# A sort and its roots one step earlier, a batch of keys behind a sum, and a different last pair, in a graph-attention kernel

## The chip, the core and the metric

The kernel runs on one core of a Trainium2 chip. The metric is the device time of one launch in microseconds (us). One execution of the program was taken by the hardware profiler; all durations of single instructions come from it.

The engines are called as the profile calls them: PE is TensorE's matmul pipeline and PEld its weight loads, DVE is VectorE, ACT is ScalarE, POOL is GpSimd, and SP is SyncE, which here only issues DMAs. A name such as L985 is line 985 of the kernel before.

## What is computed

The layer takes 2708 rows `x` of 1024 numbers and a 0/1 adjacency matrix `adj` of 2708 x 2708, in which about four entries of a row are one.

```python
h = maximum(layernorm(x), 0)
q = h @ Wq.T + bq ;  k = h @ Wk.T + bk ;  v = h @ Wv.T + bv
z = (q @ k.T) / sqrt(1024) * adj
z = where(z == 0, -10000, z)
out = x + relu(softmax(z, axis=1) @ v)
```

Since a row has few neighbours, the kernel computes no dense scores. It finds the indices of the ones in each row of `adj`, gathers the neighbours' rows of `h`, scores them one by one, and forms the weighted sum `u` of the gathered rows. The two weight matrices of the scores are combined once, M = Wq^T Wk (scaled), so that a query row is h M and its score with a neighbour is a dot product with that neighbour's h; the values' product is taken last, on the sum u.

## The kernel before, in words

**Tiles.** The rows form 22 tiles of 128 (`NT` = 22); the last, tile 21, has 20 rows and is called the rest tile. `EARLY` = 11 divides them: tiles 0 to 10 are the first part, 11 to 21 the second. Within each part the rows are sorted by their number of neighbours, so that a tile of the sorted order needs as many gathers as its longest row. A "row tile" below is a tile in sorted order; the table `ptab` holds, for each sorted row, its neighbours' indices and its own number in `x`.

**Matmul units.** After the combination of the weights (to about 105 us), TensorE works through 20 units, each for two tiles: units 0 to 9 form queries, of tiles (0,1), (2,3), (4,5), (6,7), (8,9), and then (11,12) to (19,20); tile 10's query stands alone after unit 4. Units 10 to 19 form output rows from u, in the order (8,7), (6,5), (4,3), (2,0), (1,9), (15,14), (13,12), (16,17), (20,10), (18,19); tile 11's output stands alone at the end (`alone`). A unit (`multiply`, L940) multiplies the two tiles' 256 rows by a 1024 x 1024 matrix as seven products of half-size blocks instead of eight (a Strassen form, which costs block sums ahead and behind). Its operands are transposes of the rows (TensorE, L355), copies of these (ACT, L645: a11, a12, a22) and block sums (DVE L649, or POOL where that is named: s1 to s4). Its results are c11, c22, c12 and c21, taken from PSUM: for queries by L982 (ACT), L985 and L988 (DVE sums) and L993 (ACT); for outputs by L1010 to L1026, where ACT applies the relu. Copies of partial products that later products are added to are L917, L920 and the like on ACT. The first two products of unit n+1 are issued inside unit n (`opened`), ahead of its last.

**Hooks.** Between the products of unit n the code calls `after(0)` to `after(6)`. There the next unit's rows, transposes and block sums are issued, and there the preparation of later tiles is woven in: the dictionary `steps_at` (L696) lists, by (unit, hook), short steps that `follow` (L270) carries out:

- s: statistics of tiles (DVE, L212); r: the root, eight small GpSimd instructions that form scale and bias from them (L232 to L239); a: the normalisation with relu, applied in place (ACT, L248)
- h: the rows' store to HBM (`h_dram`, GpSimd's queue, L255) and their addition to a running sum (GpSimd, L257); k: the store with the addition left for later; +: that addition
- p: "size", a pass of ACT over a tile's adjacency rows that counts its ones (L320); it also makes the next load into that buffer possible, as there are three
- f: the index search in a tile's adjacency (DVE, four instructions of L330); i, j: search, and the keys of a batch of four tiles (`listed`, L332 on; DVE L342 and those after it); e: size, search and keys; here an f for the batch's last tile is not given its keys
- c: counts of neighbours in the first part, up to a table of hot bits by degree (DVE, L595 to L603); o: the sort of the first part, two matmuls against constant matrices, a scan and some sums on DVE (L606 to L622), which gives each row its place
- w: one indirect DMA for each of tiles 0 to 10 puts the rows' table entries into their places in HBM (GpSimd, L564), and the table is read back (L576)

The second part's counts and sort stand in unit 3's hooks 2 and 3 (L1126 to L1130), without letters; `entered` then puts its eleven entries, reads the table back and gathers tiles 11 and 12 of h (L541), the rows for unit 5's queries. The second sort's result is also needed for the attention stream.

**Attention.** A generator (`attention`, L850) yields after each small piece, and `advance` pulls pieces in proportion to the matmuls issued. For each row tile it asks for the neighbours' rows (`ask`, `fill`: gathers of GpSimd, L541, into a set of buffers), fetches the query rows (L543), scores (DVE L785), forms weights, and sums (DVE L838). If `near(t)` holds, because the tile's output unit is at most two units away, u stays on chip (`held`); otherwise it is stored to `u_dram` (L847) and read again by `load_rows` (L1070).

**Outputs.** `add_x` adds the rows of x to a finished output tile with an indirect DMA of GpSimd (L1003), and `scatter` writes them to their rows of the output (L739). The rest tile has been sorted behind tile 20, and its output is one row repeated (tile 20's last), which goes through a row of HBM (`tail_dram`, L1021) to `tail` (L1041): load, add x, scatter. For tile 11 (L1226 on) x is gathered ahead into y, DVE adds the relu of its product to y, and two half-row scatters write it (L1219).

**Order of instructions.** ACT and DVE issue in program order until unit 5, from there DVE alone; GpSimd does so until step w, where `pooled.close()` ends it. The other engines, and these outside those stretches, are ordered by a scheduler that goes by dependencies and priorities; `tc.issue_after(x)` holds what stands under it behind instruction x. So where a step's instructions land is read from each engine's order of instructions, not from the source alone. SP and POOL each issue DMAs from their own queue, in their own order.

The lines of the steps, where unit 1 is tiles (2,3) and its successor, unit 2, is tiles (4,5):

```python
(1, 4): "r8 e15",
(1, 6): "f16", (2, 1): "f17 c", (2, 2): "p16 a8", (2, 3): "h8 f18 p17",
(2, 4): "o s10 p18", (2, 5): "f19 r10 w", (2, 6): "f20 f21 a10 k10 p19",
...
def near(t):
    return any(t in unit[1:] for unit in units[:now[0] + 3] if unit[0] == "o")
```

Of the kernel before, what the change touches and what calls it, by code (L numbers as in the profile page):

```python
# [15 lines left out]
ALU = mybir.AluOpType  # L16
AX = mybir.AxisListType

P = 128
# [4 lines left out]
SLOTS = 16  # L24
# [33 lines left out]
def tile_preln_masked_attention(  # L58
# [157 lines left out]
    def moments(t):  # L216
# [4 lines left out]
        nc.scalar.activation(junk, xs[i], AF.Copy, scale=-1.0 / (ROOT * D), accum_out=mv[:, i, 0:1])  # L221
        nc.scalar.activation(junk, xs[i], AF.Square, scale=1.0 / ROOT, bias=mv[:, i, 0:1], accum_out=mv[:, i, 1:2])

    def root(first):

        group, xs, mv = normed.pop(first)
        G = len(group)
        r = stat.tile([P, 5, 4], FT, tag="r", name="r")
        mean, var = mv[:, :G, 0], mv[:, :G, 1]
        down = float(ROOT) if first < LIGHT else -1.0  # L230
        eng = nc.gpsimd
        eng.tensor_scalar(r[:, 0, :G], var, EPS, None, op0=ALU.add)  # L232
        eng.tensor_tensor(r[:, 1, :G], r[:, 0, :G], minus[:, :G], op=ALU.pow)
        eng.tensor_tensor(r[:, 2, :G], r[:, 0, :G], r[:, 1, :G], op=ALU.mult)
        eng.tensor_tensor(r[:, 2, :G], r[:, 2, :G], r[:, 1, :G], op=ALU.mult)
        eng.tensor_scalar(r[:, 2, :G], r[:, 2, :G], -0.5, 1.5, op0=ALU.mult, op1=ALU.add)
        eng.tensor_tensor(r[:, 3, :G], r[:, 2, :G], r[:, 1, :G], op=ALU.mult)
        eng.tensor_scalar(r[:, 2, :G], mean, down, None, op0=ALU.mult)
        eng.tensor_tensor(r[:, 4, :G], r[:, 2, :G], r[:, 3, :G], op=ALU.mult)  # L239
        normed[first] = group, xs, r  # L240

    def apply(first, only=range(4)):
# [27 lines left out]
    def follow(steps):  # L270

        for step in steps.split():
            first, *only = step[1:].split(".")
            first, *last = first.split("-")
            first = int(first or 0)
            if step[0] == "s":
                stats(range(first, int(last[0] if last else first) + 1))
            elif step[0] == "m":
                moments(first)
            elif step[0] == "r":  # L280
                root(first)
            elif step[0] == "a":
                apply(first, *[range(int(o[0]), int(o[-1]) + 1) for o in only])
            elif step[0] in "hk":
                keep(first, step[0] == "h")
            elif step[0] == "+":
                owe(first)
            elif step[0] == "p":
                counted(first)
            elif step == "c":  # L290
                counts(0, EARLY)
            elif step == "o":
                sort(0, EARLY)
            elif step == "w":
                pooled.close()
                with tc.issue_after(put(0, EARLY).ins):
                    back.append(reload(0, EARLY))
            else:
                if step[0] == "e":
                    counted(first)  # L300
                if step[0] != "j":
                    found(first)
                if step[0] != "i":
                    listed(first)
# [372 lines left out]
    def natural_rows(n):  # L677
# [16 lines left out]
    nc.vector.tensor_scalar(large[:, 1:2], large[:, 1:2], 250000.0 / D, None, op0=ALU.is_gt)  # L694

    steps_at = {(0, 0): "s4-5 e9", (0, 1): "r4 +0 +1 +2 f10", (0, 3): "p10 i11", (0, 4): "j11 a4 p11", (0, 5): "h4 +3 s6-7 e12",  # L696
                (0, 6): "r6 f13", (1, 1): "f14", (1, 2): "p13 a6", (1, 3): "h6 s8-9 p14", (1, 4): "r8 e15",
                (1, 6): "f16", (2, 1): "f17 c", (2, 2): "p16 a8", (2, 3): "h8 f18 p17",
                (2, 4): "o s10 p18", (2, 5): "f19 r10 w", (2, 6): "f20 f21 a10 k10 p19", (3, 2): "p20", (3, 3): "p21"}

    slots, free = [], []

# [145 lines left out]
        done.add(t)  # L848

    def attention(order):  # L850
        for t in order[:3]:
            ask(t)

        fill()
# [33 lines left out]

    def near(t):

        return any(t in unit[1:] for unit in units[:now[0] + 3] if unit[0] == "o")

    def advance(us):

# [110 lines left out]
    def o_results(ta, tb):  # L1005
        ya = work.tile([P, D], FT, tag="q", name=f"y_{ta}", bufs=4)
        yb = work.tile([P, D], FT, tag="q", name=f"y_{tb}", bufs=4)

        def c11(X):
            nc.scalar.activation(ya[:, lo], X, AF.Relu)  # L1010
# [14 lines left out]
        def c21(Y):  # L1025
            nc.scalar.activation(yb[:, lo], Y, AF.Relu)  # L1026
            send(add_x(yb, tb))
            sent.append((yb, tb))

        return c11, c22, c12, c21  # L1030

# [9 lines left out]
    def tail(t):  # L1041
        n = tiles[t][1]
        y = work.tile([P, D], FT, tag="q", name=f"y_{t}", bufs=4)
        nc.sync.dma_start(y[:n], tail_dram.to_broadcast([n, D]))
        add_x(y, t, n)
        scatter(y, t, n)
# [67 lines left out]
    for n, unit in enumerate(units):  # L1114
# [8 lines left out]
        results = (q_results if kind == "q" else o_results)(ta, tb)  # L1123

        def after(i):
            if (n, i) == (3, 2):  # L1126
                counts(EARLY, NT)
            if (n, i) == (3, 3):
# [38 lines left out]
                follow(steps_at[n, i])  # L1167
            if (n, i) == (3, 4):
                searched()
            if nxt is None and i == 1:  # L1170
                while alone not in done:
                    advance(1.0)
                r, = load_rows(("o", alone))
                single["turned"] = turned(r, "alone")
# [50 lines left out]

    y = work.tile([P, D], FT, tag="q", name="y_alone", bufs=4)  # L1226
    send(gather(y, x, alone, SLOTS, P))
    tail(NT - 1)
    uT, (X, Z), p1 = single["turned"], single["banks"], single["first"]
    add_block(Z, uT[:, 0:4, :], T[:, 0])  # L1230
    add_block(Z, uT[:, 4:8, :], M[:, 1, 1])
# [188 lines left out]
```

## Time and profile before

| what | value |
|---|---|
| time, median of 3 runs (lowest to highest) | 678.27 us (677.11 to 678.88) |
| the profiled execution: time, span in the profile | 678.58 us, 676.8 us |
| mean granted clock of TensorE over the span | 0.991 |
| instructions | 6390 |
| TensorE's products (L904), the two largest groups | 320 matmuls each, 145.3 us and 144.1 us |
| gathers of neighbours' h (POOL L541) | 104, 124.6 us |
| scores (DVE L785), sums (DVE L838) | 112.6 us, 98.7 us |
| index search (DVE L330) | 88 instructions, 74.4 us |
| HBM | 161.38 MB read, 45.46 MB written, 306 GB/s over the span |

How to read it. The page's first part gives, for each engine, how long it was busy and the share of the span. A list of waits has lines of the form "waiting instruction <- what ended its wait: us, number of waits, longest"; the left side is the engine, its operand and its line, the right side the releaser. A table of stretches has a row for each window "from:to" in us from the span's start: its length, then each engine's busy time with the number of instructions, then TensorE's granted clock (1.00 is full speed), the share of the DMA engines in use, and GB/s. A listing in order of time has the start, the duration, the engine, the line, the operation, its output and inputs with their shapes, and in brackets the idle time of that engine before it with its releaser. "Issue" as a releaser means that nothing the profile shows was waited for.

The slices of the page, 40 of 16.9 us each, give the course of the whole:

```profile
PE   7999999998998999999999999999999999999894
POOL 2559990756475764576656265775684776862123
PEclk9999999999999999999999999999999999999898
```

Each digit is a busy share in tenths, and 9 is 90% or more. TensorE's dips after the first slice lie in slices 10, 13, 38 and in the last.

### The profile page before, as it was taken

The numbers are of one execution on the slowest core, as the hardware profiler recorded it, in microseconds if no ns is written. First come the engines' busy times: TensorE is split into PE (matmuls) and PEld (weight loads), VectorE is DVE, ScalarE is ACT, GpSimd is POOL, SyncE is SP. The second block draws the span as 40 slices with busy tenths as digits, with TensorE's granted clock in tenths as the row PEclk, the third lists the DMA queues.
The fourth block names the chain that finished last, engine by engine and source line by source line (L and its number), as shares of the span: only waits on it lengthen the run. The fifth ranks groups of instructions, "written<-read, shape, count | busy, mean of one in ns | idle before, by whom it ended". The sixth has DMA issues, their size and how long they took to land.

```text
span 676.8 us, 6390 instructions
## 1 busy us (share of the span) xinstructions
PE 655.5 (97%) x1768; PEld 334.8 (49%) x1768; DVE 525.7 (78%) x1010; ACT 266.3 (39%) x399; POOL 402.1 (59%) x397
## 2 busy tenths in 40 slices
PE   7999999998998999999999999999999999999894
PEld 4777765443544444444444444444444444444441
DVE  5999879989798402999878999788799989989001
ACT  3467985673727212243241232342322343332210
POOL 2559990756475764576656265775684776862123
PEclk9999999999999999999999999999999999999898
DMA  8997989698464997699899999998997899883534
GB/s 343 407 367 258 369 308 373 220 403 292 161 243 152 380 329 294 201 367 313 302 335 357 374 414 382 300 311 254 312 294 199 241 316 309 250 277 81 162 99 137
DMA packets 62452, 194.29 MB, mean 287 GB/s; under 512 B 9721, under 2 KB 10073, under 8 KB 61514
## 3 DMA queue, kind: packets, MB, share of 16 engines
q0 software_dynamic: 34608, 109.77, 49.9%
q1 hardware_dynamic: 26794, 80.89, 32.2%
q10 hardware_dynamic: 1008, 3.15, 1.2%
q8 instruction: 16, 0.26, 0.1%
q14 instruction: 26, 0.21, 0.1%
HBM read 161.38 MB, written 45.46 MB: 306 GB/s over the span
## 4 chain that ended last, share of the span: by engine, by line
PE 74%; DVE 10%; DMA 7%; issue 4%; ACT 3%; POOL 1%; POOLq 0%; ACTq 0%; SPq 0%; DVEq 0%
PE ps L904 32%; PE psy L904 23%; PE ps_y L414 6%; PE ps_x L414 4%; PE ps_z L414 4%; PE pt L355 4%; DMA adj<-in_adj_dram 3%; DVE u L838 2%; DVE at L330 2%; DVE junk L785 1%; DVE s L649 1%; DMA y<-in_x_dram,tab 1%; ACT sized L320 1%; DMA u_dram<-u 1%; DMA out_dram<-y,tab 1%
## 5 line engine op out<-in xcount | busy, mean ns | idle before, releaser
L541 POOL DMA_INDIRECT g<-h_dram,tab x104 | 124.6, 1198 | 51.3 <-issue 22.8
L904 PE MATMUL psy<-wlow,s 128*128 128x512 f32 x320 | 145.3, 596 | 0.0
L904 PE MATMUL ps<-M,a 128*128 128x512 f32 x320 | 144.1, 593 | 0.1
L785 DVE SCALAR_TENSOR_TENSOR junk<-g,pq 128x1024 uint8<-128x1024 f32 x92 | 112.6, 1223 | 2.0
L838 DVE SCALAR_TENSOR_TENSOR u<-g,coef,u 128x1024 f32<-128x1024 f32 x77 | 98.7, 1282 | 8.9 <-ACT u L830 7.3
L904 PEld LDWEIGHTS psy<-wlow,s 128*128 128x128 f32 x320 | 59.8, 192 | 67.4 <-issue 67.4
L904 PEld LDWEIGHTS ps<-M,a 128*128 128x128 f32 x320 | 59.3, 190 | 68.0 <-issue 67.7
L904 PE MATMUL psy<-wlow,a 128*128 128x512 f32 x160 | 73.9, 606 | 3.1 <-DVE q L985 2.7
L330 DVE FIND_INDEX8 at<-ones,adj 128x8 uint32<-128x685 f32 (+1 forms) x88 | 74.4, 864 | 0.0
L904 PE MATMUL ps<-M,s 128*128 128x512 f32 x160 | 71.9, 592 | 0.0
L904 PE MATMUL ps<-wlow,s 128*128 128x512 f32 x160 | 71.9, 592 | 0.0
L1003 POOL DMA_INDIRECT y<-in_x_dram,tab x21 | 37.2, 1769 | 57.9 <-ACT y L1018 28.4
L320 ACT ACTIVATE sized<-adj 128x2708 uint8<-128x2708 f32 (+1 forms) x22 | 54.2, 2464 | 7.2 <-DMA adj<-in_adj_dram 7.1
L904 PEld LDWEIGHTS psy<-wlow,a 128*128 128x128 f32 x160 | 30.7, 194 | 43.5 <-issue 35.9
L904 PEld LDWEIGHTS ps<-wlow,s 128*128 128x128 f32 x160 | 30.4, 190 | 38.3 <-issue 38.0
L904 PEld LDWEIGHTS ps<-M,s 128*128 128x128 f32 x160 | 30.3, 190 | 37.3 <-issue 37.3
L257 POOL TENSOR_TENSOR hsum<-hsum,x 128x1024 f32<-128x1024 f32 (+1 forms) x17 | 40.3, 2370 | 0.4
L649 DVE TENSOR_TENSOR s<-a,pt 128x512 f32<-128x512 f32 x40 | 25.6, 680 | 17.2 <-ACT a L645 9.7
L543 POOL DMA_INDIRECT pq<-q_dram,tab x11 | 15.5, 1411 | 33.2 <-DVE junk L785 21.2
L645 ACT COPY a<-pt 128x512 f32<-128x512 f32 x60 | 33.2, 593 | 4.2 <-PE pt L355 4.2
L541 POOL DMA_INDIRECT M<-h_dram,tab x20 | 25.9, 1293 | 11.1 <-issue 4.9
L739 POOL DMA_INDIRECT out_dram<-y,tab x21 | 24.5, 1164 | 9.8 <-issue 5.8
(229 smaller groups left out, 888.6 us busy)
## 6 DMA issues: line engine op xcount, KB each, us to landing
adj<-in_adj_dram SPq DMA_DIRECT2D x21, 1354.0 KB
x<-in_x_dram SPq DMA_DIRECT2D x21, 512.0 KB
h_dram<-x POOLq DMA_DIRECT2D x21, 512.0 KB
u_dram<-u POOLq DMA_DIRECT2D x15, 512.0 KB
or<-u_dram SPq DMA_DIRECT2D x15, 512.0 KB
q_late<-q SPq DMA_DIRECT2D x10, 512.0 KB
pq<-q_late POOLq DMA_DIRECT2D x10, 512.0 KB
g<-in_wv_dram SPq DMA_DIRECT2D x16, 256.0 KB
```

Source lines behind the costliest of these rows:

```text
L257: nc.gpsimd.tensor_add(hsum[:n], hsum[:n], xt[:n])
L320: nc.scalar.activation(sized[:n], a[:n, :, :PW], AF.Abs, accum_out=total[:n, t:t + 1])
L330: nc.vector.max_index(at[:n, t - first_t, g, :], ones[:n, 0:8], a[:n, g, :])
L355: nc.tensor.transpose(pt[:, c, :], xt[:, k * P:(k + 1) * P], ident)
L414: mm = nc.tensor.matmul(bank, a_tile(o + H * a[0], a[1], i), b(o), start=first and o == 0, stop=(o == H - 1), skip_group_check=True)
L541: return nc.gpsimd.indirect_dma_start(out=dst, out_offset=None, in_=src, in_offset=off, bounds_check=N - 1, oob_is_err=False)
L645: nc.scalar.copy(ops[name], bank)
L649: step = (eng or nc.vector).tensor_tensor(ops[name], a, b, op=op)
L785: chained(lambda: nc.vector.scalar_tensor_tensor(junk, g_of[t][s], 1.0, tq[t], op0=ALU.mult, op1=ALU.mult, accum_out=zall[:, t, s:s + 1]))
L838: chained(lambda: nc.vector.scalar_tensor_tensor(u, g_of[t][s], coef[:, at[t][s]:at[t][s] + 1], u, op0=ALU.mult, op1=ALU.add))
L904: mm = nc.tensor.matmul(bank, a[:, c, :], b[:, c, :], start=False, stop=(c == 3), skip_group_check=True)
L1003: return nc.gpsimd.indirect_dma_start(out=y[:n], out_offset=None, in_=x, in_offset=off, compute_op=ALU.add)
```

## The change

The change has five parts.

1. **The sort of the first part stands earlier, and the roots ahead of the entries.** The counts (c) move from hook (2,1) to (1,6), and the sort with tile 10's statistics (o s10) from (2,4) to the beginning of hook (2,2), through a new dictionary `steps_ahead`, so that they stand ahead of what else that hook issues. Tile 10's root (r10) moves from (2,5) to (2,3), and step w from (2,5) to (2,3), behind the index search of tile 18 and the size of tile 17. `h8` moves behind w in the same hook. Tile 10's apply (a10) moves from (2,6) to (2,4), ahead of the size of tile 18, and its store (k10) to (2,5). `root` notes its last instruction in `rooted`, and w issues the eleven entries behind the last root noted, and the reload behind the last entry.
2. **The keys of a batch stand behind a sum.** Step e15 (size, search and keys) becomes p15 and i15 in hook (1,4), and the keys (j15) come a hook later, in (1,5). Between the two stands the sum L985 of that unit.
3. **The attention stream asks for the gathers of its first two tiles at once, not of three.** The third is asked for when the stream comes to it.
4. **Tile 11's u stays on chip.** `near` is true for `alone`, so that neither the store to `u_dram` nor the load takes place.
5. **The last pair and the rest tile.** For the last output pair, tiles 18 and 19, x is gathered into ya and yb ahead of the products, one DVE instruction for each quarter of the result takes the relu of it and adds x, and the scatters follow directly; ACT's relus and the adding DMAs go. `tail`, for the rest tile, is called in hook 3 of the unit behind the one that holds tile 20, which is unit 19, and not after unit 19's end.

The arithmetic of every tile is the same otherwise.

```diff
@@ -221,6 +221,8 @@
         nc.scalar.activation(junk, xs[i], AF.Copy, scale=-1.0 / (ROOT * D), accum_out=mv[:, i, 0:1])
         nc.scalar.activation(junk, xs[i], AF.Square, scale=1.0 / ROOT, bias=mv[:, i, 0:1], accum_out=mv[:, i, 1:2])
 
+    rooted = []
+
     def root(first):
 
         group, xs, mv = normed.pop(first)
@@ -236,7 +238,7 @@
         eng.tensor_scalar(r[:, 2, :G], r[:, 2, :G], -0.5, 1.5, op0=ALU.mult, op1=ALU.add)
         eng.tensor_tensor(r[:, 3, :G], r[:, 2, :G], r[:, 1, :G], op=ALU.mult)
         eng.tensor_scalar(r[:, 2, :G], mean, down, None, op0=ALU.mult)
-        eng.tensor_tensor(r[:, 4, :G], r[:, 2, :G], r[:, 3, :G], op=ALU.mult)
+        rooted.append(eng.tensor_tensor(r[:, 4, :G], r[:, 2, :G], r[:, 3, :G], op=ALU.mult))
         normed[first] = group, xs, r
 
     def apply(first, only=range(4)):
@@ -293,7 +295,9 @@
                 sort(0, EARLY)
             elif step == "w":
                 pooled.close()
-                with tc.issue_after(put(0, EARLY).ins):
+                with tc.issue_after(rooted[-1].ins):
+                    entry = put(0, EARLY)
+                with tc.issue_after(entry.ins):
                     back.append(reload(0, EARLY))
             else:
                 if step[0] == "e":
@@ -694,9 +698,10 @@
     nc.vector.tensor_scalar(large[:, 1:2], large[:, 1:2], 250000.0 / D, None, op0=ALU.is_gt)
 
     steps_at = {(0, 0): "s4-5 e9", (0, 1): "r4 +0 +1 +2 f10", (0, 3): "p10 i11", (0, 4): "j11 a4 p11", (0, 5): "h4 +3 s6-7 e12",
-                (0, 6): "r6 f13", (1, 1): "f14", (1, 2): "p13 a6", (1, 3): "h6 s8-9 p14", (1, 4): "r8 e15",
-                (1, 6): "f16", (2, 1): "f17 c", (2, 2): "p16 a8", (2, 3): "h8 f18 p17",
-                (2, 4): "o s10 p18", (2, 5): "f19 r10 w", (2, 6): "f20 f21 a10 k10 p19", (3, 2): "p20", (3, 3): "p21"}
+                (0, 6): "r6 f13", (1, 1): "f14", (1, 2): "p13 a6", (1, 3): "h6 s8-9 p14", (1, 4): "r8 p15 i15", (1, 5): "j15",
+                (1, 6): "f16 c", (2, 1): "f17", (2, 2): "p16 a8", (2, 3): "r10 f18 p17 w h8",
+                (2, 4): "a10 p18", (2, 5): "f19 k10", (2, 6): "f20 f21 p19", (3, 2): "p20", (3, 3): "p21"}
+    steps_ahead = {(2, 2): "o s10"}
 
     slots, free = [], []
 
@@ -848,7 +853,7 @@
         done.add(t)
 
     def attention(order):
-        for t in order[:3]:
+        for t in order[:2]:
             ask(t)
 
         fill()
@@ -888,7 +893,7 @@
 
     def near(t):
 
-        return any(t in unit[1:] for unit in units[:now[0] + 3] if unit[0] == "o")
+        return t == alone or any(t in unit[1:] for unit in units[:now[0] + 3] if unit[0] == "o")
 
     def advance(us):
 
@@ -1005,6 +1010,8 @@
     def o_results(ta, tb):
         ya = work.tile([P, D], FT, tag="q", name=f"y_{ta}", bufs=4)
         yb = work.tile([P, D], FT, tag="q", name=f"y_{tb}", bufs=4)
+        if (ta, tb) == o_pairs[-1]:
+            return ends(ya, ta, yb, tb)
 
         def c11(X):
             nc.scalar.activation(ya[:, lo], X, AF.Relu)
@@ -1026,6 +1033,32 @@
             nc.scalar.activation(yb[:, lo], Y, AF.Relu)
             send(add_x(yb, tb))
             sent.append((yb, tb))
+
+        return c11, c22, c12, c21
+
+    def ends(ya, ta, yb, tb):
+
+        send(gather(ya, x, ta, SLOTS, P))
+        gather(yb, x, tb, SLOTS, P)
+
+        def joined_x(y, cols, a):
+            nc.vector.scalar_tensor_tensor(y[:, cols], a, 0.0, y[:, cols], op0=ALU.max, op1=ALU.add)
+
+        def c11(X):
+            joined_x(ya, lo, X)
+
+        def c22(Y, p5):
+            nc.vector.tensor_add(p5, Y, p5)
+            joined_x(yb, hi, p5)
+
+        def c12(Z, u2):
+            nc.vector.tensor_add(u2, Z, u2)
+            joined_x(ya, hi, u2)
+            scatter(ya, ta, P)
+
+        def c21(Y):
+            joined_x(yb, lo, Y)
+            scatter(yb, tb, P)
 
         return c11, c22, c12, c21
 
@@ -1123,6 +1156,8 @@
         results = (q_results if kind == "q" else o_results)(ta, tb)
 
         def after(i):
+            if (n, i) in steps_ahead:
+                follow(steps_ahead[n, i])
             if (n, i) == (3, 2):
                 counts(EARLY, NT)
             if (n, i) == (3, 3):
@@ -1167,6 +1202,8 @@
                 follow(steps_at[n, i])
             if (n, i) == (3, 4):
                 searched()
+            if i == 3 and units[n - 1][0] == "o" and NT - 2 in units[n - 1][1:]:
+                tail(NT - 1)
             if nxt is None and i == 1:
                 while alone not in done:
                     advance(1.0)
@@ -1225,7 +1262,6 @@
 
     y = work.tile([P, D], FT, tag="q", name="y_alone", bufs=4)
     send(gather(y, x, alone, SLOTS, P))
-    tail(NT - 1)
     uT, (X, Z), p1 = single["turned"], single["banks"], single["first"]
     add_block(Z, uT[:, 0:4, :], T[:, 0])
     add_block(Z, uT[:, 4:8, :], M[:, 1, 1])
```

## The prediction

> **What bounds the kernel.** I read the busy shares first, then TensorE's own waits, then the clock in short stretches around each wait, then each engine's order of time there.
>
> ```profile
> PE 655.5 (97%) x1768; PEld 334.8 (49%) x1768; DVE 525.7 (78%) x1010; ACT 266.3 (39%) x399; POOL 402.1 (59%) x397
> ```
>
> TensorE is busy 97% of the span, and the chain that ended last is TensorE for most of it. The change takes no matmul away, so it can win only TensorE's idle time, clock lost behind that idle time, and what follows the last matmul. TensorE's list of waits has three of over 1 us that the change can reach:
>
> ```profile
> PE psy L904 <- DVE q L985: 2.7, 1, 2.7
> PE pt L355 <- DMA or<-u_dram: 2.6, 1, 2.6
> PE ps_in L611 <- ACT a L645: 2.0, 1, 2.0
> ```
>
> The stretches around them (us; then busy time of PE, PEld, DVE, ACT, POOL; granted clock; DMA share; GB/s):
>
> ```profile
> 163.00:166.00 3.00, 0.31 (x2) 0.14 (x2) 2.76 (x17) 0.58 (x1) 1.48 (x7) 1.00 1.00 354
> 166.00:170.00 4.00, 4.00 (x6) 1.70 (x7) 4.00 (x11) 0.00 (x0) 0.00 (x0) 0.57 0.42 163
> 206.00:209.00 3.00, 0.97 (x5) 0.67 (x5) 2.21 (x11) 3.00 (x6) 1.78 (x2) 1.00 0.22 26
> 630.00:634.00 4.00, 1.43 (x5) 0.39 (x4) 0.00 (x0) 1.19 (x2) 2.35 (x2) 1.00 0.65 147
> 634.00:638.00 4.00, 4.00 (x12) 2.57 (x12) 0.00 (x0) 1.17 (x2) 0.26 (x1) 0.57 0.91 228
> ```
>
> After the first and the last wait (163, 631) the granted clock falls to 0.57 for four microseconds: 0.43 x 4 = 1.7 us of matmul time lost behind each. After the 2.0 us wait (206) it stays at 1.00.
>
> The Trainium skill, "TensorE: Matmul & The Clock Gate" (Part 1), says that the array drops to half rate after at least one idle window of about 3.4 us. By that rule waits of 2.57 and 2.69 us would cost no clock, and my sum below would be 3.4 us smaller, about 670.6 us. The windows contradict it here, so the rows decide.
>
> What ended the waits, in order of time by engine:
>
> ```profile
> 160.97 1.34 DVE L342 TENSOR_TENSOR cand<-first,at 128x128 f32<-128x128 f32 x1
> 165.13 0.67 DVE L985 TENSOR_TENSOR q<-psy,p 128x512 f32<-128x512 f32 x1
> ...
> 203.37 0.21 POOL L239 TENSOR_TENSOR r<-r 128x1 f32<-128x1 f32 x1
> 203.61 1.24 ACT L248 ACTIVATE x<-x,r 128x1024 f32<-128x1024 f32 x1 [5.27 <-issue]
> ...
> 669.09 0.97 POOL L1219 DMA_INDIRECT out_dram<-y_alone,half_i  x1 [0.30 <-issue]
> ```
>
> At 163 TensorE wants the sum L985, which stands on VectorE behind the keys of a batch (160.97 to 165.13). At 206 it waits for a hot table that VectorE finishes at 208.1 and for copies on ScalarE, which had stood 5.27 us until GpSimd ended the last root at 203.58, its eight instructions strewn among eleven table entries. At 631 it waits for row tile 11, which goes to HBM (issued 623.86) and back (630.08). And the last scatter leaves GpSimd at 669.09 though its row was ready at 667.61: the rest tile's x and scatter stand ahead of it.
>
> **Part by part.** Pair 1 is tiles 2 and 3, pair 2 tiles 4 and 5, and so on. I re-add the stretch from 160 us by the rows' durations in the changed kernel's order of instructions.
>
> *Keys behind the sum.* L985 now follows the index search that ends at 160.94 and is done at 161.6; TensorE comes at 163.0. The wait goes (2.86 us from the expected start, 163.00, to the actual, 165.86) and the lost clock with it (1.71; the eight matmuls took 5.40 instead of 3.60). The keys end at 165.1, the row's own end, because their first step was held by GpSimd's sum until 162.3 anyway.
>
> *Sort one step up.* Search 16 ends at 168.5, the hot table at 170.0 (1.5 us of counts), search 17 at 173.6. TensorE reaches the sort's two matmuls at 163.0 + 3.43 + 0.87 + 3.43 = 170.7: no wait. The sort (0.4 + 0.6 + 4 x 0.4 + 0.2; its scan took 2.51 at 184.42 under GpSimd's sum, 0.57 at 212.17 without) ends at 176.4, statistics of tile 10 (1.44) at 177.9, the s of pair 3 at 179.15. GpSimd waits for that s with everything behind it: s2 1.3, store, s4 1.3, two sums of 2.36, a store, eight root steps of 0.28 to 0.72. Its root ends near 189.9, not 203.58. Entries follow: eleven of 1.0 + 0.3, from 190.2 to about 204.7, where they ended in before (204.72). So the table is not earlier; the root is, by 13.7 us.
>
> *Tile 10's apply now stands ahead on ScalarE*, before the size of tile 18 and the copy L917 that TensorE needs for pair 3. ScalarE gets there at 181.9 and waits to 190.0 (harmless until now). Then 1.2 + 2.45 + 0.6 puts the copy at 194.2; TensorE wants it at 170.7 + 0.7 + 0.87 + 5 x 3.43 + 3.43 + 0.87 = 193.75. **A new wait of 0.5 us.** Bounds: none, if the root comes 0.5 us sooner; 14.2 with the root at the old row's 203.58. I take 0.5, from the order, in which no entry stands between root steps.
>
> *The second sort* needs tile 21's adjacency rows, whose load waits for the size of tile 18 (193.6). Its 212 KB lie between loads of 80 KB (2.06) and 512 KB (3.65): 2.8 us. The worst row, 16.99 at 132.51, had the DMA full; at 194 its share was 0.11. Search 21 runs 196.5 to 199.9, keys 1.1, counts to the hot table at 202.6; TensorE is there at 202.0. **A new wait of 0.7** in place of 2.2. The next matmul starts at 203.4, where before it was 209.10: **5.7 us gained**. If the root slips by d, both waits move with it and the gain is 5.7 - d.
>
> *Does it hold?* GpSimd's list after the root is not earlier as a whole, while TensorE is. The rows of tile 11 are gathered at 241.59, and one gather took 4.35 us from issue (266.44) to use (270.79); with the gather ahead of it (1.3) they land at 247.2 by the old times. TensorE will want them at 251.2 - 5.7 = 245.5. But tile 10's h is stored before the table's reload, not after, and the first gather waited 4.24 us for exactly that store, so this list should gain 2 to 2.5 us. I take no wait; the upper bound is 1.7.
>
> *Keys asked for two tiles, not three.* Four gathers (1.0 + 0.3 each) move behind the pair rows. They land in GpSimd's idle 1.95 and 4.93 us at 274.82 and 281.56, before tile 6 is scored near 284. Nothing gained or lost on TensorE; without that cover, at most 5.2 us on GpSimd.
>
> *Last tile on chip.* The row sum ends at 622.5 and TensorE's transposes need it at 631.1. Store, load and wait go: 2.73 (631.14 to 633.87) plus the clock, 1.71: **4.4 us**. Nothing else stands there.
>
> *Last pair's x on VectorE.* Six VectorE instructions of 0.69 in place of two; VectorE idles 20.3 us from 625.9. The sum L1013, for which TensorE's last quarter waits, keeps its place. The x gathers stand on GpSimd early, in its 11.38 us and 6.88 us idle. With the rest tile a pair earlier, the last scatter follows its row: issue at 667.8 instead of 669.09, **1.3 us**. Bounds: 0, if the tail is bound by landing, to 2.5, if the scatters ahead also slowed it.
>
> *Sum.* 5.7 + 4.4 + 1.3 = 11.4. The profiled execution took 678.58 (span 676.8 + 1.8), 0.3 above the median of the three. 678.6 - 11.4 = **667.2 us**.
>
> **Rivals.** (a) *The waits are moved more than removed.* The root comes 2 to 3 us later than I add it up, or tile 11's rows bind. The new wait then passes 2.5 us and costs clock: 2 to 3 + 1.7, so 669.2 to 672. For it: ScalarE stands idle eight microseconds ahead of that copy. Against: the sort leaves VectorE with GpSimd quiet. (b) *More.* Neither new wait shows, and the last scatter lands sooner: 11.4 + 1.2 + 1.2, about 664.8. (c) *Slower.* ScalarE's copy waits for the root as late as it came before, at 203.58: apply, size and copy to 208.0, a wait of 14.2 and 1.7 of clock, which hides the second sort's; the matmul after that sort starts at 218.1, not 209.1: +9.0, less the tail's 5.7, is +3.3 or 681.9. It decides from a root end at 200.3 (5.7 us of loss in front). Against it: every root step stands ahead of the first entry in the order. (d) *The changes don't arrive*: VectorE's 78% binds in the second half and eats the front's gain, leaving the tail's 5.7: 672.9. Against: VectorE's scoring starts from the single query, which TensorE makes, and moves with it; TensorE waits only 0.4 us for VectorE there (at 575). (e) *The clock falls all the same*, its half-rate stretches not belonging to those two waits: the gaps alone are won, 11.4 - 2 x 1.7 = 8.0, 670.6. Against: each stretch begins where its wait ends. The Trainium skill's rule on idle windows, above, has this result by leaving those two waits unpunished.
>
> **Numbers.** Forecast 0.60; (a) 0.18; (b) 0.08; (d) 0.05; (e) 0.04; (c) 0.03; 0.02 for no change. Differences under 0.3% (2 us) can't be told from none. All but (c) and the last are faster: 0.95, of which I leave 0.01 to each side for what I have not seen. The range takes (b) and most of (a): 664.6 to 671.5.
>
> **What would show it.** TensorE's waits list L990 or L985 and or<-u_dram no longer; the clock stays 1.00 from 20 us to the end; ScalarE's apply of tile 10 starts near 190; the matmul after the second sort starts near 203.4; the last scatter is issued within 0.3 us of its row. Wrong would be a TensorE wait on L917's copy beyond 2.5 us, on tile 11's gathered rows, or on VectorE after 270.

## The result, and the profile after

| | time, median (lowest to highest) | profiled execution: time, span | clock |
|---|---|---|---|
| before | 677.69 us (674.4 to 678.88, 6 runs) | 678.58, 676.8 us | 0.991 |
| after | 669.73 us (668.59 to 671.01, 6 runs) | 670.24, 668.4 us | 0.993 |

The ratio is 0.989, with a 95% interval of 0.9864 to 0.9916. The forecast was 667.2, so the time is 2.5 us over it. It counted from the profiled execution: of its gain of 11.4 us, the two profiled spans show 8.4. All line numbers behind this point are those of the kernel whose profile is shown; the changed kernel's lie 2 to 37 higher than those of before.

Busy shares of the page after the change:

```profile
PE 653.6 (98%) x1768; PEld 334.0 (50%) x1768; DVE 526.0 (79%) x1014; ACT 264.3 (40%) x395; POOL 401.4 (60%) x396
```

TensorE's list of waits after the change:

```profile
PE ps_y L453 <- POOL hsum L119: 2.8, 1, 2.8
PE ps_in L615 <- DVE hot L604: 2.2, 1, 2.2
PE ps_x L418 <- DMA wlow<-in_wq_dram: 0.8, 1, 0.8
PE psy L909 <- DVE p L1020: 0.4, 1, 0.4
```

The waits for L985 (here L990) and for the reloaded rows of tile 11 are gone, as forecast. The wait at the second sort is not: 2.2 us, where before it was 2.0. The stretches around it, and the place where tile 11's wait had been:

```profile
198.00:202.00 4.00, 3.81 (x12) 1.55 (x10) 3.83 (x13) 0.58 (x1) 3.29 (x4) 1.00 0.64 199
202.00:204.00 2.00, 0.00 (x0) 0.00 (x0) 1.59 (x8) 0.46 (x1) 0.89 (x2) 1.00 0.68 265
204.00:208.00 4.00, 3.97 (x8) 2.17 (x9) 3.87 (x8) 4.00 (x7) 0.69 (x2) 0.59 0.17 26
208.00:212.00 4.00, 4.00 (x10) 1.71 (x9) 2.23 (x7) 2.54 (x3) 3.08 (x4) 0.98 0.49 140
634.00:638.00 4.00, 4.00 (x11) 1.73 (x10) 0.69 (x1) 0.59 (x1) 0.98 (x1) 1.00 0.51 193
```

From 201.8 to 204.0 TensorE is idle, and the four microseconds behind it have a mean clock of 0.59, which had not happened behind the 2.0 us wait before. At 634 the clock is 1.00, where it was 0.57. The last scatter is issued at 660.83, 0.28 us behind its row, as forecast.

**The account.** I set the starts of the same products of TensorE against each other in the two traces. After minus before is +0.1 us at 160, -4.5 at 187, -4.3 at the first product behind the second sort, -2.6 from 213 to 627, and -7.1 at tile 11's first product (642.27 against 649.33). From that product's start to the end of the span it is 26.1 us against 27.5. So the span's 8.4 us are 2.6 from the front, 4.45 from tile 11 and 1.3 from the end.

### The profile page after: what moved, and what is told of

It is laid out like the page before. It is cut to its first block, busy times and chain, and to the rows that moved or that the text cites. A ratio compares the mean times of both kernels' runs of the same rounds, so it can differ in the third digit from the quotient of the medians.

```text
span 668.4 us, 6383 instructions
## 1 busy us (share of the span) xinstructions
PE 653.6 (98%) x1768; PEld 334.0 (50%) x1768; DVE 526.0 (79%) x1014; ACT 264.3 (40%) x395; POOL 401.4 (60%) x396
## 4 chain that ended last, share of the span: by engine, by line
PE 79%; issue 5%; DMA 5%; DVE 5%; POOL 4%; ACT 2%; POOLq 0%; SPq 0%; DVEq 0%; ACTq 0%
PE ps L909 35%; PE psy L909 24%; PE ps_y L418 6%; PE ps_x L418 4%; PE ps_z L418 4%; PE pt L359 4%; POOL g L545 2%; DMA out_dram<-y,tab 2%; DMA adj<-in_adj_dram 2%; DVE junk L790 1%; DVE at L334 1%; POOL y L1008 1%; ACT sized L324 1%; DVE u L843 1%; DMA wlow<-in_wq_dram 1%
## 5 line engine op out<-in xcount | busy, mean ns | idle before, releaser
L909 PE MATMUL ps<-M,s 128*128 128x512 f32 x160 | 73.6, 603 | 0.0
L909 PE MATMUL psy<-wlow,a 128*128 128x512 f32 x160 | 72.1, 593 | 0.4 <-DVE p L1020 0.4
L1008 POOL DMA_INDIRECT y<-in_x_dram,tab x19 | 34.0, 1788 | 26.7 <-ACT y L1025 14.9
```

The source lines that it names most:

```text
L909: mm = nc.tensor.matmul(bank, a[:, c, :], b[:, c, :], start=False, stop=(c == 3), skip_group_check=True)
L1008: return nc.gpsimd.indirect_dma_start(out=y[:n], out_offset=None, in_=x, in_offset=off, compute_op=ALU.add)
```

## The experiments

Medians are of executions beside runs of the kernel before on the same chip; the ratio is to those. Four chips were used (e1 to e4; e5, e6 and e8; e9 to e11; e12), on which the kernel before had medians of 676.95 to 678.04 us, so between chips a microsecond is read from the ratios, not from the medians.

| label | median (lowest to highest), us | ratio [95% interval] | span of the profile, us |
|---|---|---|---|
| e1_keys | 676.20 (674.51 to 679.30) | 0.9993 [0.9973, 1.0014] | 672.9 |
| e2_sort | 677.18 (673.96 to 680.60) | 1.0001 [0.9974, 1.0029] | 676.6 |
| e3_alone | 673.93 (670.79 to 676.82) | 0.9959 [0.9937, 0.9980] | 674.8 |
| e4_tail | 673.80 (671.37 to 676.28) | 0.9958 [0.9934, 0.9982] | 674.4 |
| e5_late | 669.62 (668.52 to 671.53) | 0.9891 [0.9860, 0.9921] | 668.5 |
| e6_three | 670.80 (669.98 to 671.21) | 0.9904 [0.9875, 0.9932] | 668.8 |
| e8_among | 677.26 (675.75 to 677.81) | 1.0005 [0.9988, 1.0022] | 674.1 |
| e9_late2 | 666.78 (665.86 to 666.99) | 0.9844 [0.9819, 0.9868] | 664.2 |
| e10_nosort | 670.57 (669.93 to 671.64) | 0.9902 [0.9879, 0.9924] | 668.6 |
| e11_keys2 | 676.19 (one execution) | | 674.5 |
| e12_late_nosort | 666.27 (665.98 to 666.65) | 0.9842 [0.9805, 0.9878] | 664.3 |

### One part at a time

**e1 and e11, the keys alone.** Of the line of steps, the entries that differ:

```diff
-(1, 4): "r8 e15",
+(1, 4): "r8 p15 i15", (1, 5): "j15",
```

> The kernel before with one part of the change alone: the keys of the batch behind the sum. Theory A (the front's gain is this part's alone; the sort's place buys nothing, because the second sort's table is reached along a chain of VectorE, of sizes on ScalarE and of adjacency loads that starts with TensorE's products and moves with them): the wait at 163 and its half-clock stretch go, everything up to the second sort comes 4.5 us earlier, TensorE still waits about 2.0 us there; 4.5 us less in the profile, 673.5 to 674, or 1.7 more where that wait costs clock. Rival B (without the earlier sort and root the old chain over GpSimd's entries and the root at 203.6 stays where it was, and the won time is waited off at the second sort): a wait of over 4 us there, a gain of under 1.5 us, 677 or more.

> The kernel of e1 once more, for its waits. In e1's profile TensorE waited 2.28 us at the second sort and the span was 3.9 us under that of before, but the median of its executions was only 1.2 us lower. Theory A (chance of the clock at two waits): waits as in e1's profile. Rival B: a longer wait at the second sort, over 3 us, in this execution.

**e2, the sort, root and entries alone.** The changed kernel with its other parts undone:

```diff
-(1, 4): "r8 p15 i15", (1, 5): "j15",
+(1, 4): "r8 e15",
...
-        for t in order[:2]:
+        for t in order[:3]:
```

and `near`, `o_results` and the place of `tail` as before.

> The kernel before with the sort, root and entry part alone; the keys stay ahead of the sum, and the end is as before. Theory A: the wait at 163 of 2.7 us and its clock stay; sizes and loads of the last adjacency tiles hang on TensorE's products as before, so the hot table of the second sort comes at 208 as before, TensorE waits about 2 us for it, and the time is that of before within 1 us (677 to 679). Rival B (the step of the sort is what gained): the matmul after the second sort starts 2 us or more earlier than 209.1, 676 or less.

TensorE's waits at the second sort, read from its order of time (arrival is the start less the wait):

| kernel | arrives | waits | goes on |
|---|---|---|---|
| before | 206.33 | 2.03 | 208.36 |
| e2: sort part alone | 205.46 | 2.12 | 207.58 |
| e1: keys alone | 202.02 | 2.28 | 204.30 |
| e11: keys alone, again | 202.26 | 2.52 | 204.78 |
| e10: after without the sort part | 201.88 | 2.36 | 204.24 |
| after | 201.81 | 2.22 | 204.03 |

With the keys alone both the arrival and the table come 4 us earlier, and so does the root (199.29 for 203.57). With the sort part alone the arrival moves by 0.9 us, but not through the sort. These are e2's matmuls behind the wait for the sum, and VectorE's search of tile 20:

```profile
166.69 3.70 PE L909 MATMUL psy<-wlow,a 128*128 128x512 f32 x8 [2.45 <-DVE q L990]
```

```profile
196.74 0.09 DVE L334 MATCH_VALUE_LOAD at<-ones,adj 128x8 f32 x1 [2.86 <-DMA adj<-in_adj_dram]
```

The eight matmuls took 3.70 us here and 5.40 before: in this execution that wait cost no clock, 1.7 us, and it ended 0.8 later than before. So theory A holds in the traces: **in the profiled executions the gain of the front is the keys'**, since the root and VectorE's list hang on TensorE's earlier products and follow them.

The medians do not confirm its size. e2's is that of before, as expected. e1's is 1.2 us lower, not 4, and its interval ends at 1.8; the waits of its two profiles are theory A's, the median is nearer to rival B's "under 1.5". So the 4 us rest on two profiled executions (spans 3.9 and 2.3 us lower than before's). By the medians e1 to e4 won 1.2, 0.3, 3.5 and 3.6 us, together 8.6, where the whole change won 8.0; no run takes the keys alone out of the changed kernel. Two things scatter the executions. One is the clock, in steps of 1.7 us (below). The other is the length of waits that a part leaves alone: for the sum L985 (e2's L990) it is 2.45 in e2, 2.69 before, 2.76 in e4 and 3.31 in e3. Why some executions of e1 take over 678 us no profile here shows; it stays open.

**e3, tile 11 on chip alone.**

```diff
-        return any(t in unit[1:] for unit in units[:now[0] + 3] if unit[0] == "o")
+        return t == alone or any(t in unit[1:] for unit in units[:now[0] + 3] if unit[0] == "o")
```

> The kernel before with tile 11's sum kept on chip, nothing else. Theory A: the wait of 2.6 us at 631 and 1.7 us of clock go: 4.4 us less, 673.9 against 678.3. Rival: the held buffer delays a gather of the last tiles, or the store and load shared the DMA with something that now lands no sooner; a gain of under 3 us, with a new wait in TensorE's list behind 600.

Median 673.93, 3.5 us lower, and no wait over 1 us behind 211. No cost of the held buffer shows.

**e4, the last pair and the rest tile alone** (`ends` and the earlier `tail` put into the kernel before).

> The kernel before with the last pair's x on VectorE and the rest tile a unit earlier, nothing else. Theory A: only what follows the last matmul shrinks, 1.3 us less in the profile (about 677), the last scatter issued within 0.3 us of its row; TensorE's waits as before. Rival: the rest tile's transfers collide with the row of tile 11 that is still read back here, and the wait at 631 grows by 0.5 us or more: no gain, 678 or more.

From tile 11's first product to the end of the span it takes 26.3 us (648.13 to 674.4) against 27.5: the 1.2 us are there. The wait at 631 did not grow, it was 1.98. The median is 3.6 us lower, more than these 1.2, with an interval of 1.2 to 4.5; the shorter wait and its clock can account for about another microsecond (0.6 of wait, and 1.7 of clock in fewer executions), the rest is not shown.

**e6, three tiles asked for.** `order[:3]` in place of `order[:2]` in the changed kernel.

> The changed kernel with three tiles asked for at the start of the attention stream instead of two. Theory A: nothing, 669 to 670, TensorE's list of waits unchanged. Rival: the four gathers ahead of the pair rows on GpSimd make TensorE or VectorE wait between 250 and 290: 671 or more.

No new wait; the list shows 2.4 at the sort in place of 2.2. The median, 670.80, lies between theory A's 670 and the rival's 671, and most of its interval lies in that of after. Nothing measurable, as forecast.

**e10, the changed kernel without its sort part.** The steps stand as before, and the entries are no longer held behind the root:

```diff
-(1, 6): "f16 c", (2, 1): "f17", (2, 2): "p16 a8", (2, 3): "r10 f18 p17 w h8",
-(2, 4): "a10 p18", (2, 5): "f19 k10", (2, 6): "f20 f21 p19",
+(1, 6): "f16", (2, 1): "f17 c", (2, 2): "p16 a8", (2, 3): "h8 f18 p17",
+(2, 4): "o s10 p18", (2, 5): "f19 r10 w", (2, 6): "f20 f21 a10 k10 p19",
```

> The changed kernel with its first part undone: sort, root and entries in the places of the kernel before, root steps among the entries; the keys behind the sum, tile 11's sum on chip and the last pair as changed. Fewer waits of TensorE are left here than in e1, so its executions scatter less. Theory A (the sort's place buys nothing): TensorE waits 2.0 to 2.4 us at the second sort as in the changed kernel, 669 to 670.5. Rival B (with the old order the root ends late, and in most executions ScalarE's apply and copies behind it, or the last adjacency loads, come later than TensorE): a wait over 3 us there, 671.5 to 674.

670.57 against 669.73, with about the same wait (2.36). Rival B falls. The hot table ends at 204.09, against 203.89 after, but VectorE gets there by another way. With the old order it runs from 179.6 to the table without a wait over 0.25 us: its own list decides. With the new order the first sort is out of that stretch, and VectorE waits for the last adjacency rows instead (0.74 and 1.89 us after, 2.86 in e2). The work moved away came back as waits for loads.

### Where the root stands

**e8, no rule for the root.** In the changed kernel the entries are no longer held behind the last root:

```diff
-                with tc.issue_after(rooted[-1].ins):
-                    entry = put(0, EARLY)
+                entry = put(0, EARLY)
```

> The changed kernel without the rule that puts the table entries behind the last root: eight entries then stand ahead of the root's first step and its steps alternate with the rest. Theory A (where the root stands decides, through ScalarE's apply, the size of tile 18 and the copy behind them): the root ends near 197 instead of 187.7, TensorE waits some 7 us for ScalarE's copy near 194 and loses 1.7 us of clock, while the wait of 2.2 us at the second sort goes: 4 to 6 us slower than the changed kernel, 673 to 676. Rival (the earlier table and the idle ScalarE make up for it): within 1 us of the changed kernel.

TensorE's waits of e8, and ScalarE and GpSimd around 196 in their order of time:

```profile
PE psy L908 <- ACT psy L921: 6.3, 1, 6.3
...
PE ps_in L614 <- ACT q L986: 0.6, 1, 0.6
```

```profile
196.32 1.24 ACT L250 ACTIVATE x<-x,r 128x1024 f32<-128x1024 f32 x1 [14.65 <-POOL r L241]
197.47 2.45 ACT L323 ACTIVATE sized<-adj 128x2708 uint8<-128x2708 f32 x1
...
199.91 0.57 ACT L921 COPY psy<-ps 128x512 f32<-128x512 f32 x1
```

```profile
191.75 1.01 POOL L567 DMA_INDIRECT tab_dram<-tab,pos_i  x1 [0.16 <-issue]
192.79 0.20 POOL L239 TENSOR_TENSOR r<-r 128x1 f32<-128x1 f32 x1
...
196.09 0.19 POOL L241 TENSOR_TENSOR r<-r 128x1 f32<-128x1 f32 x1
```

The root ends at 196.3, ScalarE stands 14.65 us, and TensorE waits 6.3 us for the copy behind apply and size. The span is 5.7 us over the changed kernel's, as expected (4 to 6), the median 7.5, which is more; the mechanism is the forecast's rival (c), with its place and its releaser. So the rule for the root is needed, but only because this change puts the apply ahead of that copy. With the old order (e10) the copy stands ahead of the apply and the late root harms nobody.

### The wait that was left

**e5, the second sort one product later.** TensorE has eight matmuls right behind the sort's two that do not need them:

```diff
-            if (n, i) == (3, 3):
-                with tc.issue_after(products[-1].ins):
-                    placed.append(sort(EARLY, NT))
-                entered()
...
-        add_block(Z, ops["s4"], M[:, 1, 1])
+        behind_it = add_block(Z, ops["s4"], M[:, 1, 1])
+        if n == 3:
+            with tc.issue_after(behind_it.ins):
+                placed.append(sort(EARLY, NT))
+            entered()
```

> The changed kernel with the second sort's two matmuls one product later on TensorE (behind the eight matmuls that stood behind them). Theory A (the forecast missed 3 us because VectorE's hot table of the second sort comes at 203.9 while TensorE is there at 201.8, and because this wait of 2.2 us costs clock in about half of the executions): TensorE has 3.4 us of other work in that place, the wait and the half-clock stretch go, nothing behind is later: span about 664.5 in the profile (668.4 - 2.2 - 1.7), time 666 to 667, with little spread. Rival (the sort's result is then late for what follows, tile 11's rows or the attention stream): a wait of the same size later, 669 to 670.

The wait at the sort went, and another came. TensorE's list, and GpSimd ahead of the second part's entries:

```profile
PE pt L359 <- DMA qr<-h_dram,tab: 2.5, 1, 2.5
```

```profile
209.57 1.02 POOL L545 DMA_INDIRECT M<-h_dram,tab  x1 [0.30 <-DVE bad L709]
210.59 2.74 POOL L721 MEMSET g<- 128x1024 f32 x3
213.50 1.44 POOL L545 DMA_INDIRECT g<-h_dram,tab  x1 [0.17 <-POOL g L721]
215.24 1.16 POOL L568 DMA_INDIRECT tab_dram<-tab,pos_i  x1 [0.30 <-issue]
```

The places (`pos_i`) were ready at 208.7, but the first entry starts at 215.24 (after: 209.6 and 210.65): the scheduler had pulled three clears and a gather ahead, and tile 11's rows, the forecast's other half of rival (a), came 2.5 us late. 669.62 us, nothing won.

**e9, the same with GpSimd's order kept.**

```diff
-        for i in range(8, HIGH):
-            nc.gpsimd.memset(slots[i], 0.0)
+        with tc.issue_after(puts[1][-1].ins):
+            for i in range(8, HIGH):
+                nc.gpsimd.memset(slots[i], 0.0)
```

> The changed kernel with the second sort's matmuls one product later, as in e5, and with the three clears of buffers held behind the second part's table entries, so that GpSimd's entries, reload and gathers of tile 11's rows keep the order that they have in the changed kernel. Theory A (the wait that came up in e5 for tile 11's rows was GpSimd's order, 4.2 us of clears and a gather ahead of the entries, not the later sort): no wait of TensorE over 1 us between 20 us and the end, the clock at 1.00 there in every execution; 2.2 us less than the changed kernel's undisturbed executions of 668.6, so 666 to 667, spread under 1.5 us. Rival (the table is too late for tile 11's rows whatever GpSimd's order): a wait on these rows near 244, 668 to 670.

```profile
209.66 1.01 POOL L545 DMA_INDIRECT M<-h_dram,tab  x1 [0.30 <-issue]
210.98 1.28 POOL L568 DMA_INDIRECT tab_dram<-tab,pos_i  x1 [0.30 <-DVE g L731]
```

The first entry stands at 210.98, near its place in the changed kernel, and TensorE's list holds no wait over 0.4 us behind the first 20 us:

```profile
PE ps_y L453 <- POOL hsum L119: 2.8, 1, 2.8
PE ps_x L418 <- DMA wlow<-in_wq_dram: 0.8, 1, 0.8
PE psy L910 <- DVE p L1025: 0.3, 1, 0.3
```

**666.78 us**, 3 us under the changed kernel, and the executions lie within 1.1 us of each other, against 2.4 after and 4.5 before. This beats both kernels.

**e12, e9 without the change's sort part.**

> The kernel of e9 with the change's first part undone, as in e10: the sort of the first part, tile 10's root and the entries stand where they stood before; the second sort's matmuls still come one product later. No wait over 1.95 us is left to chance here, so a microsecond can be seen. Theory A (the first part bought nothing that TensorE sees; the second sort's table comes when the last adjacency loads let it): 666.3 to 667.3, as e9's 666.78. Rival (the earlier root and the earlier first table bring the second part's entries and tile 11's rows forward, and TensorE needs that once it no longer waits at the sort): a wait for tile 11's rows near 244 or for ScalarE's copies near 205, 668 or more.

666.27 us, ratio 0.9842 against e9's 0.9844. Where the executions of a kernel lie within about a microsecond, **no gain of the earlier sort, root and entries is seen**, though the hot table comes at 202.70 in e9 and at 204.32 in e12: with the matmuls one product later, neither keeps TensorE waiting.

### What an idle microsecond does to the clock

**e7, trains of matmuls with idle times between.** No part of the layer is computed. One execution, of 3690.94 us, was profiled.

```python
for _ in range(24 + (turn * 3 + k) % 5):
    nc.tensor.matmul(bank, weights, wide[:, :NB], start=True, stop=True)
nc.vector.tensor_scalar(wide[:, :1], bank[:, :1], 0.0, None, op0=ALU.mult)
nc.vector.tensor_tensor(wide[:, :w], wide[:, :w], zeros[:, :w], op=ALU.add)
```

> No part of the computation: the output is zeros. Trains of 24 to 28 matmuls of 128x512, and between two trains TensorE waits for one VectorE instruction of 0.7 to 3.4 us, 14 lengths, ten times each at shifting times. It measures which idle time is followed by half-rate matmuls. Theory A (a window that runs freely, of some 3.4 us, judges TensorE by its share of work in it, so a gap well under the window is judged by chance of its place): no stretch behind gaps under about 1.7 us, some behind gaps from 2 to 2.6, nearly all behind gaps over 3. Rival 1 (a fixed length of the gap decides): none below a sharp limit between 2.03 and 2.57 us, all above it. Rival 2 (only a whole idle window counts): none below 3.4 us.

TensorE in its order of time; the bracket is the idle time ahead of a train, and each product gives two matmul records:

```profile
106.63 24.30 PE L78 MATMUL bank<-wide,weights 128*128 128x512 f32 x56 [1.80 <-DVE wide L80]
132.94 22.56 PE L78 MATMUL bank<-wide,weights 128*128 128x512 f32 x48 [2.01 <-DVE wide L80]
...
265.64 20.87 PE L78 MATMUL bank<-wide,weights 128*128 128x512 f32 x48 [3.05 <-DVE wide L80]
...
399.44 20.87 PE L78 MATMUL bank<-wide,weights 128*128 128x512 f32 x48 [1.17 <-DVE wide L80]
```

48 matmuls take 20.87 us behind 1.17 us of idle time, and also behind 3.05; behind 2.01 they take 22.56, 1.7 more. So the length of the gap does not decide. Of ten gaps of each length, this many were followed by half rate in the trace's record of the granted clock:

```
gap, us    1.17 to 1.80   2.01  2.22  2.42  2.63  2.84  3.05  3.26  3.47  3.68  3.88
half rate      0 of 40       7     8     3     5     7     4    10     8     8     9
by chance         0         4.4   5.0   5.6   6.2   6.8   7.5   8.1   8.7   9.3   9.9
```

Every half-rate stretch starts on one grid of 3.413 us and lasts one period of it, or two. Cut by this grid, the trace has 959 periods at full rate behind 106 us: none with up to 1.947 us of idle time in it was followed by half rate, each with 1.973 or more was. (The ends of matmuls are modelled in the profile; the limit is as sharp as that model.) The last line of the table is what follows from that for a gap that falls anywhere on the grid: (3.413 - 1.96 + gap - 1.96) / 3.413 of the time the part of it in one period passes 1.96. It sums to 71 for the hundred gaps of over 2 us, and 69 were counted. The same limit holds in all other profiles here, where the longest idle time in one full-rate period that half rate did not follow is 1.90 us and the shortest that it did follow is 2.06: the 2.03 us wait of before had been cut by the grid into 1.14 and 0.89, the 2.22 us wait of after lay whole in one period. Theory A holds, with its limit at 1.96 us (its "nearly all over 3" was too much: of ten gaps of 3.05 us four were caught); both rivals fall.

This also tells a part of why executions scatter. Before had waits of 2.69, 2.03 and 2.57 us, which are caught with chances of 0.64, 0.45 and 0.60, at 1.7 us each: 2.9 us on average, between 0 and 5.1. After has one, of 2.2 us: 0.9 on average. Its executions fall into two groups accordingly: three of 668.6 to 669.2 us with a mean clock of 0.997 or 0.998 over the span, three of 670.2 to 671.0 with 0.993 to 0.995. The kernel before spread over 6.7 us in the 35 executions beside e1 to e4, more than 5.1, so the clock is not all of it.

## Why the prediction was right, and where it was off

*Mechanism and most sizes right.* The keys behind the sum: 4.57 us forecast, 4.65 measured at the products behind it. Tile 11 on chip: 4.4 forecast, 4.45 measured. The end: 1.3 forecast, 1.3 measured. Three tiles or two: nothing forecast, nothing measurable. VectorE's second half took nothing back: -2.6 us stays constant from 213 to 627, so rival (d) is out. Rival (e) is out with the clock of 1.00 from 163 to 170 and at 634, and "slower" (c) with ScalarE's apply at 187.70.

*The step that failed is "the second sort: a new wait of 0.7".* It came out as 2.2, and this wait cost 1.65 us of clock in the profiled execution. That is 1.5 + 1.65 = 3.2 us, less 0.2 by which TensorE came there sooner than forecast: the 3.0 that the span misses (11.4 forecast, 8.4 measured). VectorE in order of time, after the change:

```profile
192.95 0.09 DVE L334 MATCH_VALUE_LOAD at<-ones,adj 128x8 f32 x1 [1.89 <-DMA adj<-in_adj_dram]
...
196.45 0.19 DVE L346 TENSOR_TENSOR cand<-first,at 128x32 f32<-128x32 f32 x1
...
197.54 0.06 DVE L334 MATCH_VALUE_LOAD at<-ones,adj 20x8 f32 x1
...
203.52 0.37 DVE L604 TENSOR_TENSOR hot<-deg,down 128x198 f32<-128x198 f32 x1 [0.28 <-DVE deg L603]
```

I had looked at tile 21's rows and priced their load. What came last was tile 20: its rows let the search begin at 192.95, 1.1 us of keys follow (196.45 to 197.54), which my sum left out as if search 21 could begin when its own rows were there, and only then search 21. The hot table ends at 203.89, where I had 202.6. Which load comes last varies. In e5 and e9 the search of tile 20 begins at 190.95 and 191.57 and the table ends at 202.4 and 202.7; in e6 VectorE waits another 1.36 us for tile 21's own rows, the ones that I had priced, and the table ends at 204.3.

*The root was costed too late, and it did not matter.* It ended at 187.66, where I had 189.9, since the first hot table ended at 168.35 and not at 170.0, and GpSimd began pair 3's sum at 176.84 and not at 179.15; so the forecast wait of 0.5 on ScalarE's copy did not appear. The forecast set a root earlier "by 13.7 us" and 1.1 us of gain (5.7 less the keys' 4.57) on the sort part. e10 and e12 show no gain of it. Before, VectorE's table (208.21) and ScalarE's copies behind the late root (208.24) came within 0.03 us of each other, and the list names the copies; but in every profile in which TensorE waits there it goes on 0.14 to 0.15 us behind the end of the table, and in e2 the earlier root (191.34) left a wait of 2.12.

*The clock.* I read the rows, in which waits of 2.57 and 2.69 us cost clock and one of 2.03 did not, as a limit on the length of a wait. It was chance of place. The Trainium skill's page "TensorE: Matmul & The Clock Gate" (Part 1) gives a window of 3413 ns that runs freely, and e7's grid agrees with both. Part 1 of that page of the Trainium skill also has the rate fall after at least one idle window of about 3.4 us, and its section "Why this matters for your kernels" warns of gaps over about 3 us; e7 agrees with neither: 1.97 us of idle time within one period were enough, and a gap of 3.05 us that the grid cut in two cost no clock.

*The result landed in rival (a)'s range by another cause, so that part of the range was right by luck.* (a) had the front's wait pass 2.5 us because the root or tile 11's rows came late. The wait was VectorE's table, and 2.2 us were enough. That tile 11's rows stand close behind was right: e5 shows them binding with 4.2 us more on GpSimd.

## What to carry to other kernels

Where TensorE waits for an engine's list, re-add that list to its end from the operand that arrives last, every tile's keys included, and not only from the operand that the change touches. If the matmuls that wait have others behind them that don't need the result, exchange them before anything else: here it gave 3 us, where no gain of the rearranged chain ahead was seen; but look in every queue at what the scheduler moves along. Count a wait of about 2 us or more at its length plus 1.7 us times the chance that one clock period holds 1.96 us of it; by this estimate, which no run here tried, two waits of 1.9 us in different periods, 3.8 in all, cost less than one of 3, which is 4.2 on average.

## What the hardware did that I had not expected

Half-rate stretches of exactly 3.413 us, on a fixed grid, triggered by 1.96 us of idle time within one period (57%), not by a gap's length. While a stretch lasts, less is enough to keep it: of 90 such periods in e7, those with up to 0.57 us idle were followed by full rate, those with 0.62 or more by another half-rate period. Both limits say nearly the same if the work done counts at the granted rate: (3.413 - 1.96) / 3.413 = 0.43 at full rate, 0.5 x (3.413 - 0.6) / 3.413 = 0.41 at half rate. That last reading is argued, not shown.
